# A two-layer graph kernel: copies out of PSUM planned on either of two engines, layer 1's sums put elsewhere, GpSimd's deviations ranked first, and the verdict taken earlier

## The chip, the core and the metric

The kernel runs on one core of one Trainium2 chip. A core has a matrix engine (TensorE, in the profile PE, with its weight loads as PEld), a vector engine (VectorE, DVE), a scalar engine (ScalarE, ACT), a slower general engine (GpSimd, POOL) and SyncE (SP), which here issues nearly all DMA transfers. Each engine works through its own queue in order; semaphores tie the queues together. Matmul results land in PSUM, a small memory[...], from which ScalarE or VectorE copies them to SBUF.

The metric is the device time of one launch in microseconds. It was measured in three runs; separately, one execution was profiled.

## The reference, cut to what matters

There are 3327 nodes with 256 features. Layer 0 makes two steps of top-p attention and of a propagation with the given dense matrix, layer 1 is a graph attention with four heads over the non-zeros of that matrix.

```python
h = jnp.maximum(_layernorm(x, axis=-1), 0.0)
# layer 0, h is X
R = S + jnp.eye(N); R = R / R.sum(-1, keepdims=True)
Xf = X; Xa = X; Z = 0
for n in range(2):
    A = _top_p_attention(Xa, W1, W2, W3)      # softmax, nucleus 0.9, renormalised
    Xf = R @ Xf
    Xa = A @ Xa
    Z = Z + Xf @ U1[n].T + Xa @ U2[n].T
x = x + layernorm(X + Z) * ln_g + ln_b
# layer 1, on h = relu(layernorm(x)):
hp = (h @ W).reshape(n, H, FH)
e = leaky_relu(s[:, :, None] + d[:, None, :], 0.2)   # s, d: hp with the two halves of a
attn = softmax(where(adj > 0, e, -inf), axis=2)
x = x + elu(einsum('hij,jhf->ihf', attn, hp))
```

## The kernel before

The nodes are cut into 26 tiles of 128 rows. Everything is float32. A function `fast` does the work with a quick search for the nucleus threshold, and sets a flag `again` where its assumptions fail; a slow function `general` then runs instead. With the inputs here it does not run.

**How the order comes about.** `fast` does not issue its instructions as it goes. It describes pieces of work to a `Plan`: for each piece an engine, a length in microseconds, a rank, the pieces that it needs, and buffers that it takes and gives back. `Plan.order` (from L496) then walks through a simulated time: each engine, when free, starts that ready piece with the lowest rank whose buffers are free. `Plan.issue` writes the instructions out in the order found, so the order of every engine's queue is fixed when the kernel is built. The chip follows that order; only its waits are found at run time.

**The stages.** First each tile of x is loaded and normalised. `deviations` (from L1133) measures mean and variance on VectorE (L1142, L1143) and takes the reciprocal deviation for a group of one to four tiles on GpSimd (L1147 to L1150); `prepare` applies it on ScalarE (L1168), transposes the tile on TensorE (L1173), copies it (L1176), projects it to keys and queries (L1181), copies that to `kq` (L1187) and spreads it with two GpSimd copies (L1190, L1191) and an SP transfer (L1194). `project_u` (L1220) multiplies each tile by the first layer weights.

Each of the two steps n then does, for each of 26 rows of tiles: logits (L882) and exponentials (L893); a search for the threshold by counting passes over 3327 columns on ScalarE (L930) with small steps on GpSimd or VectorE; a window and sort on VectorE (L985, L990); four drops (L1042); and `attention`: seven groups of up to four transpositions (L1055) into a two-deep PSUM buffer `px`, a copy to SBUF by ScalarE (`Row.turned`, L1060), and matmuls into `acca` (`Row.attend`, L1067). After the first step `finish1`, after the second `finish2`, carry the row on; each turns its result on TensorE and copies it to `xt` by ScalarE (L1242, L1360), and `finish1` copies `kq` (L1251).

Beside this, `Full` multiplies the loaded matrix tiles with the features, 26 matmuls for each row of tiles (L1099), into `accf`. ScalarE copies the sum out (`Full.copy`, L1106), and `Full.add` (L1115) adds the row's own tile on VectorE. In the first step there is one `accf` buffer; in the second there are two, the halves of one PSUM bank. These matmuls depend on no search, so they fill TensorE's time.

Layer 1, `attend_neighbours`, works in four quarters of columns (W = 832). For each of 26 tiles j it makes masks on ScalarE (L1634, L1635), four exponents on VectorE (L1646) into an `e` buffer, and matmuls into PSUM (L1662 for the features, L1676 for the sums). At the end of a quarter `leave` copies the sums out (L1724, L1727) into one of the four `e` buffers, and they are transposed (L1746), divided and stored.

After the plan, written out by hand, the verdict closes: reductions of the failure marks (L1925 to L1929) and two times a copy, a transposition (L1936) and a reduction (L1937), then the flag (L1938). All engines load the flag (L1945) and branch past `general`.

```python
if j == 0 and self.n == 0:
    self.acc = ps_a.tile([P, D + 1], F32, name="accf")
elif j == 0:
    if self.t == 0:
        late["accf"] = ps_a.tile([P, 2, D], F32, name="accf")
    self.acc = late["accf"][:, self.t % 2, :]
```

Of the kernel before, what the change touches and what calls it, by code (L numbers as in the profile page):

```python
# [25 lines left out]
H = 4  # L26
# [443 lines left out]
class Plan:  # L470
# [8 lines left out]
    def put(self, engine, length, rank, fn, *args, needs=(), take=(), give=(), lag=None, hold=0.0):  # L479
# [7 lines left out]
        while stack:  # L487
            q = stack.pop()
            if isinstance(q, dict):
                p["needs"].append(q)  # L490
                q["then"].append(p)
            elif q is not None:
                stack.extend(q)
        self.pieces.append(p)
        return p

    def order(self):
# [11 lines left out]
        for k, p in enumerate(self.pieces):  # L509
            p["k"], p["left"], p["from"] = k, len(p["needs"]), 0.0  # L510
            if not p["left"]:
                ready[p["engine"]].append(p)
        out, clock, holds = [], 0.0, []
        while len(out) < len(self.pieces):
            while events and events[0][0] <= clock:
# [14 lines left out]
                for q in p["then"]:  # L530
                    if (q["engine"] == p["engine"]) == (what == "own"):
                        q["left"] -= 1
                        if not q["left"]:
                            ready[q["engine"]].append(q)
            for e, queue in ready.items():
# [6 lines left out]
                queue.remove(p)  # L542
# [30 lines left out]
def fast(  # L573
# [59 lines left out]
    with ExitStack() as l0:  # L633
# [215 lines left out]
        plan = Plan(dict(rows=1, mvs=3, pl=2, px=2, acca=1, accf=1, accf0=1, accf1=1, et=3, at=4, y=1, e2=3, mask=2, **BUFS))  # L849

        class Row:
# [205 lines left out]
            def turned(self, g):  # L1057
                m = min(4, NT - 4 * g)
                self.et[g] = etpool.tile([P, 4, P], F32, name="et")
                S.copy(self.et[g][:, :m, :], self.pt.pop(g)[:, :m, :])  # L1060
# [16 lines left out]
        class Full:  # L1077


            def __init__(self, n, t):  # L1080
                self.n, self.t, self.at = n, t, {}
                self.src, self.w = (main, D + 1) if n == 0 else (c, D)
                self.bank = f"accf{t % 2}" if n else "accf"
# [6 lines left out]
            def some(self, js):  # L1090
                for j in js:
                    if j == 0 and self.n == 0:
                        self.acc = ps_a.tile([P, D + 1], F32, name="accf")
                    elif j == 0:

                        if self.t == 0:
                            late["accf"] = ps_a.tile([P, 2, D], F32, name="accf")
                        self.acc = late["accf"][:, self.t % 2, :]
# [5 lines left out]
            def copy(self):  # L1104
                self.f = small.tile([P, H * FH + 2 * H], F32, name="f", bufs=BUFS["f"])
                S.copy(self.f[:, : self.w], self.acc[:, : self.w])  # L1106

# [4 lines left out]
            def add(self):  # L1112
                rs = rsum[:, self.t : self.t + 1]
                f, here = self.f[:, :D], c[:, self.t, :]
                V.tensor_add(f, f, self.src[:, self.t, :D])  # L1115
# [17 lines left out]
        def deviations(lo, hi):  # L1133
# [23 lines left out]
            a = plan.put("POOL", 1.1 + 0.2 * m, -100.0 + lo, rest, needs=[a])  # L1157
            return {lo + k: (a, held, k, k == m - 1) for k in range(m)}

        def prepare(t, measured):  # L1160
# [24 lines left out]
            def share():  # L1185
                held["kq"] = small.tile([P, P], F32, name="kq", bufs=BUFS["kq"])
                S.copy(held["kq"], held["ps"])  # L1187
# [9 lines left out]
            a = hs[0][t] = plan.put("ACT", 0.6, r, relu, needs=[ready_], give=["mvs"] * last)  # L1197
            a = plan.put("PE", 0.25, r, turn, needs=[a], take=["pl"])
            a = turned_h[t] = plan.put("DVE", 0.43, r, copy, needs=[a], give=["pl"])
            a = plan.put("PE", 0.5, r, project, needs=[a, weighed], take=["px"])  # L1200
            a = plan.put("ACT", 0.3, r, share, needs=[a], take=["kq"], give=["px"])
# [9 lines left out]
        def project_u(t, rank):  # L1211
# [10 lines left out]
            a = plan.put("PE", 1.75, rank, product, needs=[turned_h[t], uloads], take=[bank])  # L1222
# [5 lines left out]
        def finish1(row, done, rank):  # L1228
# [11 lines left out]
            def copy():  # L1240
                held["xt"] = small.tile([P, 2, P], F32, name="xt")
                S.copy(held["xt"], held["pt"])  # L1242
# [6 lines left out]
            def share():  # L1249
                held["kq"] = small.tile([P, P], F32, name="kq", bufs=BUFS["kq"])  # L1250
                S.copy(held["kq"], held["ps"])  # L1251
# [32 lines left out]
            x_ = plan.put("ACT", 0.3, r, copy, needs=[a], take=["xt"], give=["px", "xa"])  # L1284
            a = plan.put("PE", 0.45, r, project, needs=[x_], take=["px"])
            a = plan.put("ACT", 0.27, r, share, needs=[a], take=["kq"], give=["px"])
# [31 lines left out]
        def finish2(row, done, z, rank):  # L1318
# [39 lines left out]
            def copy():  # L1358
                held["xt"] = small.tile([P, 2, P], F32, name="xt")
                S.copy(held["xt"], held["pt"])  # L1360
# [25 lines left out]
            a = plan.put("POOL", 0.85, r, deviation, False, needs=[a])  # L1386
            a = plan.put("DVE", 1.6, r, second, needs=[a, x_], take=["mv"], give=["mv"], hold=0.95)
            s_ = plan.put("SP", 0.1, r, store, needs=[a])
            a = plan.put("POOL", 1.1, r, deviation, True, needs=[a])
# [3 lines left out]
            a = plan.put("ACT", 0.3, r, copy, needs=[a], take=["xt"], give=["px", "xa"])  # L1393
            a = plan.put("PE", 0.9, r, project, needs=[a], take=["px"])
            a = plan.put("ACT", 0.72, r, stage, needs=[a], take=["f"], give=["px", "xt"])
            return plan.put("DVE", 0.6, r, scale, needs=[a], give=["f"]), s_
# [24 lines left out]
        def search(row, rank, keys, stats_of, fresh):  # L1421
# [4 lines left out]
            for g in range(2):  # L1426

                def logits(g=g):
# [4 lines left out]
                    "PE", 2.0 - 0.8 * g, rank - 2.5, logits, needs=[keys, fresh, a], take=["pl", "pl"] + ["e", "sc"] * (1 - g)  # L1433
# [8 lines left out]
            a = row.pieces["guess"] = plan.put("ACT", 1.0, rank - 2.4, row.guess, needs=[a])  # L1442
# [542 lines left out]
```

## Time and profile before

| | us |
|---|---|
| median of three runs | 2197.55 |
| lowest and highest | 2196.28, 2198.43 |
| the profiled execution, its time | 2193.86 |
| the profiled execution, its span | 2192.1 |
| TensorE busy | 2158.7 |
| VectorE busy | 1605.3 |
| ScalarE busy | 1441.6 |
| GpSimd busy | 926.6 |

The span runs from the first to the last instruction; the time also holds what lies around it. A group row of the profile reads: line, engine, operation, tile written and tiles read, shape, count, then busy time of the group and mean nanoseconds of one, then the idle time of the engine just before these instructions and what ended it. A wait row gives total, number, longest. A timeline row gives start, length, engine, line, and in brackets the idle time before it. A float32 matmul appears as two records. The ends of matmuls are modelled, so a busy TensorE can hide short refills.

### The profile page before, as it was taken

To read this page: it belongs to the slowest core of one execution; us is meant where nothing else is said; L and a number is where in the kernel's file an instruction comes from. 1 tells how busy PE (TensorE), PEld (TensorE's weight loads), DVE (VectorE), ACT (ScalarE), POOL (GpSimd) and SP (SyncE) were. 2 spreads that over 40 slices of the span, in tenths; PEclk is the share of its full clock that TensorE was granted. 3 is DMA by queue.
4 is the path that set the end of the run, shared out by engine and by line. 5 is a ranking of instruction groups with operands and counts; after the bars stand their busy time and mean duration, and the time that the engine had idled before them with its cause. 6 is when DMAs were issued, how large, how long until landed. Compare 5 with 4: busy or idle time off the path is not lost. (4 is left out here: it accounts for less than half of the span.)

```text
span 2192.1 us, 35711 instructions
## 1 busy us (share of the span) xinstructions
PE 2158.7 (98%) x11872; PEld 1519.1 (69%) x11872; DVE 1605.3 (73%) x4205; ACT 1441.6 (66%) x2714; POOL 926.6 (42%) x2259
## 2 busy tenths in 40 slices
PE   8999999999999999999999999999999999999997
PEld 6578778778787788777778777878788433333332
DVE  5567666657556571367998888788878898989896
ACT  5786776667666742578888787788673556465553
POOL 5466565546533550265666665656563100000001
PEclk9999999999999999999999999999999999999999
DMA  4012122222222233532222222222124534444341
GB/s 121 21 36 85 48 63 62 64 72 64 57 58 62 72 116 92 154 95 58 63 59 64 59 74 61 75 75 69 56 72 136 157 114 145 119 137 127 110 127 53
DMA packets 192323, 183.74 MB, mean 84 GB/s; under 512 B 15386, under 2 KB 146176, under 8 KB 192128
## 3 DMA queue, kind: packets, MB, share of 16 engines
q1 hardware_dynamic: 191232, 181.15, 28.4%
q8 instruction: 95, 1.56, 0.3%
q14 instruction: 100, 0.82, 0.1%
q10 hardware_dynamic: 896, 0.21, 0.0%
HBM read 164.41 MB, written 15.94 MB: 82 GB/s over the span
## 5 line engine op out<-in xcount | busy, mean ns | idle before, releaser
L1067 PE MATMUL acca<-rhs,et 128*128 128x256 f32 x2704 | 618.2, 379 | 0.1
L930 ACT ACTIVATE junk<-e,sc 128x3327 fp8e5<-128x3327 f32 x182 | 558.8, 3070 | 81.4 <-POOL sc L975 81.0
L1067 PEld LDWEIGHTS acca<-rhs,et 128*128 128x128 f32 x2704 | 498.3, 190 | 61.8 <-issue 1.8
L1099 PE MATMUL accf<-c,at 128*128 128x256 f32 x1352 | 316.1, 383 | 6.3 <-ACT f L1106 5.7
L985 DVE SCALAR_TENSOR_TENSOR y<-e,sc 128x1664 f32<-128x1664 f32 x104 | 204.8, 1969 | 152.6 <-POOL sc L972 150.3
L1099 PE MATMUL accf<-main,at 128*128 128x257 f32 x1352 | 309.8, 381 | 1.5 <-ACT f L1106 1.5
L1099 PEld LDWEIGHTS accf<-c,at 128*128 128x128 f32 x1352 | 249.2, 190 | 54.1 <-issue 10.6
L1099 PEld LDWEIGHTS accf<-main,at 128*128 128x128 f32 x1352 | 251.4, 190 | 46.1 <-issue 8.1
L1060 ACT COPY et<-px 128x512 f32<-128x512 f32 (+1 forms) x364 | 192.6, 553 | 119.5 <-PE acca L1067 62.9
L990 DVE MAX8 cands<-y 128x8 f32<-128x208 f32 x832 | 242.2, 361 | 3.6
L1042 DVE SCALAR_TENSOR_TENSOR e<-e,thr 128x832 f32<-128x832 f32 x208 | 212.9, 1081 | 2.0
L893 ACT ACTIVATE e<-pl 128x1024 f32<-128x1024 f32 x208 | 179.9, 869 | 43.3 <-PE pl L882 43.3
L1635 ACT ACTIVATE et<-at 128x448 bf16<-128x448 f32 (+1 forms) x204 | 112.3, 550 | 131.9 <-DVE e L1646 74.2
L1798 POOL TENSOR_TENSOR qq<-qq 128x256 f32<-128x256 f32 x4 | 3.0, 757 | 461.2 <-ACT qq L1794 461.1
L1055 PE MATMUL px<-ident,e 128*128 128x128 f32 x1352 | 191.9, 274 | 6.0 <-ACT et L1060 3.5
L1055 PEld LDWEIGHTS px<-ident,e 128*128 128x128 f32 x1352 | 160.1, 141 | 50.0 <-issue 13.5
L1662 PE MATMUL pl<-e,main 128*64 128x416 f32 x1024 | 192.5, 517 | 0.3
L882 PE MATMUL pl<-kt,qq 64*128 64x512 f32 (+1 forms) x832 | 173.7, 536 | 0.8 <-ACT e L893 0.8
L1662 PEld LDWEIGHTS pl<-e,main 128*64 128x64 f32 x1024 | 70.9, 137 | 113.3 <-issue 86.4
L1646 DVE SCALAR_TENSOR_TENSOR e<-c,low,et 128x832 f32<-128x832 f32 x128 | 128.6, 1070 | 12.0 <-PE accf L1676 10.4
L882 PEld LDWEIGHTS pl<-kt,qq 64*128 64x128 f32 x832 | 71.5, 186 | 84.4 <-issue 77.3
L1646 DVE SCALAR_TENSOR_TENSOR e<-qq,low,et 128x832 f32<-128x832 f32 x120 | 120.4, 1072 | 6.0 <-PE accf L1676 4.4
(534 smaller groups left out, 3032.3 us busy)
## 6 DMA issues: line engine op xcount, KB each, us to landing
at<-in_adjt_dram SPq DMA_DIRECT2D x414, 256.0 KB
at<-in_adjt_dram SPq DMA_DIRECT2D x102, 192.0 KB
at<-in_adjt_dram SPq DMA_DIRECT2D x52, 128.0 KB
ys<-ystage SPq DMA_DIRECT2D x26, 256.0 KB
rhs<-in_x_dram SPq DMA_DIRECT2D x26, 128.0 KB
ystage<-in_x_dram SPq DMA_DIRECT2D x26, 128.0 KB
base<-ys SPq DMA_DIRECT2D x26, 128.0 KB
x1s<-ystage SPq DMA_DIRECT2D x26, 128.0 KB
```

What stands on the lines that cost most here:

```text
L882: T.matmul(pl[:, lo : lo + m], qq[half, self.i, :], kt[half, 512 * k : 512 * k + m], start=True, stop=True,)
L893: S.activation(self.e[:, 1024 * k : 1024 * k + pl.shape[1]], pl, AF.Exp, accum_out=(self.p0, self.p1, self.p2, self.p3)[k],)
L930: S.activation(junk[:, :N], self.e[:, :N], fn, bias=t, scale=-1.0, accum_out=dst, saturate=False)
L985: V.scalar_tensor_tensor(self.y[:, : hi - lo], self.e[:, lo:hi], self.up, self.e[:, lo:hi], ALU.is_lt, ALU.mult, accum_out=(self.h0, self. ...
L990: V.max(self.cands[:, o // PIECE, :], self.y[:, o - lo : min(o + PIECE, hi) - lo])
L1042: V.scalar_tensor_tensor(piece, piece, self.thr[:, o : o + 1], piece, ALU.is_gt, ALU.mult)
L1055: T.transpose(pt[:, k, :], self.e[:, j * P : (j + 1) * P], ident)
L1060: S.copy(self.et[g][:, :m, :], self.pt.pop(g)[:, :m, :])
L1067: T.matmul(self.acc, et[:, j - 4 * g, :], rhs[self.n][:, j, :], start=(j == 0), stop=(j == NT - 1))
L1099: T.matmul(self.acc[:, : self.w], self.at[j // JC][:, j % JC, :], self.src[:, j, : self.w], start=(j == 0), stop=(j == NT - 1),)
L1646: V.scalar_tensor_tensor(held["e"][:, k, :], extra["both"][b % 2][:, k, :], low[:, j, k : k + 1], held["mask"], ALU.max, ALU.mult,)
L1662: T.matmul(q["acc"][a][k * FH : (k + 1) * FH, c, :C], main[:, j, h * FH : (h + 1) * FH], held["e"][:, h, c * C : (c + 1) * C], start=(j == 0),
```

## The change

Most copies out of PSUM become pieces that two engines can do: `Plan.either` gives a length and a function for each of ScalarE and VectorE, and the walk through simulated time gives the piece to whichever engine gets to it first. This holds for the transposed tiles, for `xt` in `finish1` and `finish2`, for `kq` in `finish1` and for the sums of `Full`; for the last, VectorE's variant `take` adds the row's own tile in the same instruction. The copies of `kq` in `prepare` stay on ScalarE.

The second step's `accf` becomes one buffer. The rank of GpSimd's deviations goes from -100 to -180. Layer 1's sums leave PSUM into `y` (free since the last search) and the memory of `kt`, and take no `e` buffer. The verdict becomes three pieces of the plan with ranks that fall into the last quarter, with one transposition where there were two. Some thirty lengths of pieces are changed, among them those of the steps, the guess, the windows and the exponents.

```diff
+        p["on"] = {engine: (length, fn, p["lag"], hold)}
         self.pieces.append(p)
+        return p
+
+    def either(self, first, second, rank, *args, **kw):
+
+        p = self.put(*first[:2], rank, first[2], *args, **kw)
+        p["on"] = {e: (length, fn, self.LAG[e], 0.0) for e, length, fn in (first, second)}
+        p["engine"] = ""
         return p
...
                 p = min(can, key=lambda q: q["rank"])
-                queue.remove(p)
+                for k in p["on"]:
+                    ready[k].remove(p)
+                p["engine"] = e
+                p["length"], p["fn"], p["lag"], p["hold"] = p["on"][e]
...
-            def turned(self, g):
+            def turned_by_s(self, g):
+                self.turned(g, S.copy)
+
+            def turned_by_v(self, g):
+                self.turned(g, V.tensor_copy)
+
+            def turned(self, g, copy):
                 m = min(4, NT - 4 * g)
                 self.et[g] = etpool.tile([P, 4, P], F32, name="et")
-                S.copy(self.et[g][:, :m, :], self.pt.pop(g)[:, :m, :])
+                copy(self.et[g][:, :m, :], self.pt.pop(g)[:, :m, :])
...
-                    if j == 0 and self.n == 0:
-                        self.acc = ps_a.tile([P, D + 1], F32, name="accf")
-                    elif j == 0:
-
-                        if self.t == 0:
-                            late["accf"] = ps_a.tile([P, 2, D], F32, name="accf")
-                        self.acc = late["accf"][:, self.t % 2, :]
+                    if j == 0:
+                        self.acc = ps_a.tile([P, self.w], F32, name="accf")
...
+            def take(self):
+                self.f = small.tile([P, H * FH + 2 * H], F32, name="f", bufs=BUFS["f"])
+                V.tensor_add(self.f[:, :D], self.acc[:, :D], self.src[:, self.t, :D])
+                if self.n == 0:
+                    V.tensor_copy(self.f[:, D : D + 1], self.acc[:, D:])
+                self.added = True
...
-                V.tensor_add(f, f, self.src[:, self.t, :D])
+                if not self.added:
+                    V.tensor_add(f, f, self.src[:, self.t, :D])
...
-            a = plan.put("POOL", 1.1 + 0.2 * m, -100.0 + lo, rest, needs=[a])
+            a = plan.put("POOL", 1.25 + 0.19 * m, -180.0 + lo, rest, needs=[a])
...
-            x_ = plan.put("ACT", 0.3, r, copy, needs=[a], take=["xt"], give=["px", "xa"])
+            x_ = plan.either(
+                ("ACT", 0.3, copy), ("DVE", 0.43, lambda: copy(V.tensor_copy)), r, needs=[a], take=["xt"],
+                give=["px", "xa"],
+            )
...
-                a = plan.put("DVE", 2.7, rank - 1.3, row.step, 2, V, needs=[a])
+                a = plan.put("DVE", 3.35, rank - 1.3, row.step, 2, V, needs=[a])
...
-                b = plan.put("ACT", 0.03 + 0.115 * m, rank - 2.6, row.turned, g, needs=[b], take=["et"], give=["px"])
+                b = plan.either(
+                    ("ACT", 0.06 + 0.105 * m, row.turned_by_s), ("DVE", 0.12 + 0.135 * m, row.turned_by_v),
+                    rank - 2.6, g, needs=[b], take=["et"], give=["px"],
+                )
...
-                    take=[f.bank] * (j == 0) + ["accf"] * (n == 1 and t + j == 0), give=["at"] * last,
+                    take=["accf"] * (j == 0), give=["at"] * last,
                 )
-            a = plan.put(
-                "ACT", 0.3, -90.0, f.copy, needs=[a], take=["f"],
-                give=[f.bank] + ["accf"] * (n == 1 and t == NT - 1),
+            a = plan.either(
+                ("ACT", 0.35, f.copy), ("DVE", 0.45 + 0.12 * (n == 0), f.take), -90.0, needs=[a], take=["f"],
+                give=["accf"],
             )
...
-                        q["ot"] = epool.tile([P, NP], F32, name="e")[:, : 3 * W].rearrange("p (k c w) -> p k c w", k=3, c=2)
+                        q["ot"] = scr.tile([P, 2 * W], F32, name="y").rearrange("p (k w) -> p k w", k=2)
+                        q["ot"] = [q["ot"][:, 0], q["ot"][:, 1]]
                     if k < 2:
-                        S.copy(q["ot"][:, k], q["acc"][k][:, :, :C])
+                        S.copy(q["ot"][k].rearrange("p (c w) -> p c w", c=2), q["acc"][k][:, :, :C])
                     else:
+                        if "den" not in extra:
+                            extra["den"] = wpool.tile([P, 2 * W], F32, name="kt")[:, :W]
+                        q["ot"].append(extra["den"])
...
+        def gather_rows():
+            late["pr"] = ps_x.tile([1, P], F32, name="px")
+            T.transpose(late["pr"], far[:, 0:1], ident)
+
+        def tell():
+            V.tensor_reduce(verdict[:, 0:1], late["pr"], AX.X, ALU.max)
+            V.tensor_tensor(again, verdict[:, 0:1], verdict[:, 0:1], ALU.max)
+
+
+        a = plan.put("DVE", 1.5, 92.0, judge, needs=[[a for a, _ in ends], failed])
+        a = plan.put("PE", 0.15, 92.1, gather_rows, needs=[a], take=["px"])
+        plan.put("DVE", 0.45, 92.2, tell, needs=[a], give=["px"])
         plan.issue(tc)
```

## The prediction

> **What bounds the kernel now.** I read the totals first, then busy time by stage, then TensorE's own waits, then the timeline at the two kinds of wait that recur. The totals:
>
> ```profile
> span 2192.1 us, 35711 instructions
> PE 2158.7 (98%) x11872; PEld 1519.1 (69%) x11872; DVE 1605.3 (73%) x4205; ACT 1441.6 (66%) x2714; POOL 926.6 (42%) x2259
> ```
>
> TensorE is busy in all but 33.4 us of the span, at a granted clock of 0.997. The change takes one 128x128 transposition from TensorE and adds none, so the matmul stream itself, some 2159 us, stays. Whatever is won must come out of the 33.4 us, or from small refills that a busy figure hides. Where the idle time lies, by stage (columns: stretch; length; busy time of TensorE, weight loads, VectorE, ScalarE, GpSimd; clock; DMA):
>
> ```profile
> core 0: us, PE busy (x) PEld busy (x) DVE busy (x) ACT busy (x) POOL busy (x), PEclk, DMA share, GB/s
> 0.00:34.00 34.00, 27.12 (x162) 22.04 (x163) 22.02 (x77) 19.25 (x51) 23.98 (x85) 0.95 0.52 152
> ...
> 95.00:150.00 55.00, 53.26 (x279) 41.27 (x278) 40.77 (x148) 45.03 (x89) 36.23 (x79) 1.00 0.18 50
> 150.00:800.00 650.00, 648.46 (x3257) 517.38 (x3256) 405.26 (x1173) 450.54 (x788) 350.71 (x851) 1.00 0.23 66
> ...
> 915.00:1710.00 795.00, 783.77 (x3967) 637.45 (x3965) 643.34 (x2074) 602.95 (x1030) 459.52 (x1108) 1.00 0.25 72
> 1710.00:2176.00 466.00, 465.66 (x3384) 169.79 (x3384) 429.82 (x488) 249.50 (x595) 4.53 (x5) 1.00 0.43 124
> 2176.00:2192.10 16.10, 4.90 (x35) 2.47 (x27) 7.35 (x24) 6.18 (x16) 6.14 (x7) 0.71 0.18 59
> ```
>
> So: opening 6.9 us idle, 95 to 150 us 1.7, first step 1.5, second step (915 to 1710) 11.2, layer 1's quarters 0.3, end 11.2. TensorE's waits name the releasers:
>
> ```profile
> PE accf L1099 <- ACT f L1106: 7.2, 13, 1.1
> PE pl L1173 <- ACT rhs L1168: 3.6, 3, 2.5
> PE px L1055 <- ACT et L1060: 3.5, 2, 3.2
> ...
> PE px L1055 <- DVE e L1042: 1.1, 3, 0.6
> PE px L1055 <- DVE gk L789: 1.1, 1, 1.1
> ```
>
> The first and third rows are copies out of PSUM that ScalarE makes late. Two stretches show the form, TensorE first:
>
> ```profile
> 961.95 1.89 PE L1067 MATMUL acca<-rhs,et 128*128 128x256 f32 x8
> 963.68 1.03 PE L1099 MATMUL accf<-c,at 128*128 128x256 f32 x4
> 965.17 1.13 PE L1099 MATMUL accf<-c,at 128*128 128x256 f32 x4 [0.46 <-ACT f L1106]
> ```
> ```profile
> 1562.85 3.07 ACT L930 ACTIVATE junk<-e,sc 128x3327 fp8e5<-128x3327 f32 x1 [5.39 <-POOL sc L975]
> ...
> 1565.91 0.56 ACT L1060 COPY et<-px 128x512 f32<-128x512 f32 x1
> ```
>
> Eight matmuls take 961.95 to 963.68, 0.216 us each. The next four take 1.49 us where 0.86 would do: 0.63 lost (0.46 of it shown as idle). The new row of tiles writes the other half of the same bank, and still TensorE waits for the copy of the old half. In the second stretch a copy stands behind a 3.07 us count; TensorE waited 3.2 us.
>
> **The change part by part.**
>
> 1. *The sums' copy (L1106) and one buffer in the second step.* The order of the two builds shows 9 of 25 boundaries between rows of tiles in the second step with no other matmul between before, 3 after; the rest now have at least four. Before, the waits there are 7 of 0.46, 2 of 0.69 and 1.10 at 917 us, 5.7 in all. After: 3 x 0.46 = 1.4, where the three are copy 0.37 plus hand-over. Saved 4.3; and 0.17 of refill (0.63 less 0.46) at some six boundaries, 1.0. Of 52 copies 15 go to VectorE as an add straight from PSUM, which takes the place of the 0.42 us add that VectorE made anyway (two cost 0.15 more for the row sum's column in the first step): VectorE's load does not grow by them.
>  Here the Trainium skill speaks against the change: "Trace Analysis", section Optimizing Tensor Performance, Matmuls, has independent matmul groups rotate through PSUM banks, so that the copy of one lies beside the next group's matmuls. The change takes the second buffer away. By the rule every boundary would now show its copy, 0.46, and 25 of them 11.5 us, against none with rotation. By the row the two halves never rotated in effect, and the single buffer of the first step, with matmuls of other rows between, shows only 1.5 us for 26. I take the row.
>
> 2. *Transposed tiles (L1060) by either engine.* 139 of 364 copies go to VectorE (120 of 128x512, 19 of 128x256; 80 of the 139 in the second step), with 12 and 6 copies of xt and 8 of kq. The trace has no 128x512 copy on VectorE. From its PSUM copies of 64 columns (222 ns) and 256 (417 ns, L1176), 1.02 ns a column: 0.68 us, an estimate; bounds 0.42 (no cost beyond 256) and 0.83 (two of 256). ScalarE takes 584 ns. VectorE gains 120 x 0.68 + 37 x 0.42 + 8 x 0.28, about 99 us; ScalarE sheds about 92. Both lie beside TensorE. In the second step VectorE goes from 643 to about 643 + 57 = 700 of 795 us (88%), ScalarE from 603 to about 550. What is queued behind such a copy on VectorE is a row's window, sort and drops, for which that row's transpositions wait. In the new order, copies standing right behind a count on ScalarE fall from 78 of 364 to 36 of 225, and of L1106 from 28 of 52 to 11 of 37. Gain: the 3.2 us hole, and at 95 to 150 us two holes of 0.83 and 0.91 in which a copy or exponential stood behind a count: 1.4 of 1.7. In the first step 0.4 (one wait for L1106); the 1.1 for L789 stays, VectorE's own queue. Added: late drops, 0.5; and if the 165 moved copies are exposed as ScalarE's 364 were (3.5 us, 0.010 each), 1.6.
>  The unknown is how often a copy on VectorE comes late: never at best, and at worst often enough for rival three.
>
> 3. *Deviations first on GpSimd.* At the opening a group of three deviations (L1147 to L1150) ran at 17.40 behind three pairs of key copies that waited for ScalarE's kq; its inputs were there by 14.4. After, one pair stands ahead of it, done at 15.15. Its relu (19.26), and the transposition behind the 2.51 us hole, come 2.2 earlier. Keys and their kq buffers are freed up to 1.8 later per group; SP's copies of kq do not pass GpSimd. Gain 2.2, from 0 (the hole moves to the keys, which the first logits need, 51.8 us) to 4. In the new order 6 instead of 9 products L1220 stand ahead of those logits: less filler should a key be late.
>
> 4. *Layer 1's sums in y and kt.* The transposed sums no longer hold one of four e buffers. TensorE is idle 0.34 us in 1710 to 2176, so at most 0.3; I take 0. VectorE's waits there cost nothing while TensorE is full.
>
> 5. *Verdict in the last quarter.* Its five reductions (369, 149, 154, 196, 161 ns), one transposition and two small operations run under TensorE, with 36 us free on VectorE in that stage. Removed: two copies (150 each), a transposition, a reduction, and the wait: all five engines' loads of the flag start at 2185.9, right after the verdict's last write. TensorE's branch then takes 4.35 us to 2190.9, while SP branches at 2187.1 and reports from 2190.1. After, TensorE is free from 2181.6 and leaves the chain; SP, whose flag load now stands ahead of its last stores, branches after its last store at about 2185.9: 1.2, with 0.1 of VectorE's reduction ahead of the last quotient: 1.3. The output stores themselves stay.
>
> 6. *Lengths of the planner:* no instruction, only order; changes of row mode on TensorE number 1,141 in both.
>
> **Sum.** Opening 2.2, 95 to 150 us 1.4, first step 0.4, second step 4.3 + 1.0 + 3.2 - 0.5 = 8.0, end 1.3: 13.3; less 1.6 for new waits: 11.7, say 12. The profiled execution took 2193.86 (span 2192.1), below the runs shown (2196.28 to 2198.43). It would take 2181.9, with a span near 2180; the median 2197.55 becomes **2185.5**.
>
> **Rivals.**
>
> One: nearly all idle time before the last matmul goes but the 1.8 ahead of the first one. 33.4 less 9.5 behind the last matmul leaves 23.9; 19 of it and 1.3 at the end make 20: 2177.5. For it: the planner's lengths come closer to the rows (a window's first half, 1.95 + 1.2, was planned at 3.2, now 3.12; step three at 2.7 now 3.35). Against: VectorE's late drops stay.
>
> Two: the choice of engine is made when the plan is built, not when an engine is free; holes move and don't shrink. For it: the plan's fixed places, as all the waits above came out of a plan too. Gain 0 to 4, about 2195.5.
>
> Three, the other sign: VectorE in the second step. A copy there sits behind a 1.95 us window operation or a 3 us step in a queue that is 88% full; two px buffers hang on it, and TensorE, in order, stands still. Price: 139 copies; from 0.09 us exposed each the gain is gone (12.5), from 0.12 it is slower than can be taken for noise. At 0.15 (21 us): 2206. Against: ScalarE, 76% full, exposed 0.010.
>
> **How the numbers follow.** Forecast 0.70 (own range 2179 to 2192), rival one 0.11, two 0.09, three 0.10. The range reaches from 2177 to 2196: it leaves out rival three, half of two and part of one. A difference of 0.2% is 4.4 us, about what can be told from none. Faster: forecast, one, and a fifth of two, 0.83; same 0.07; slower 0.10.
>
> **What would show it.** TensorE's idle time in the second step from 11.2 to about 4; its wait for L1106 from 7.2 to about 2 in total; no wait over 3 us for a transposed copy; the hole at 17 us under 0.5; flag loads of the engines at different times, TensorE's branch over by 2187 on the old time axis. It is wrong if waits of TensorE for VectorE's copies sum to over 5 us, or if VectorE stays under 670 us in the second step. Also wrong if the 128x512 copy on VectorE takes over 0.83.

## The result, and the profile after

The changed kernel takes **2187.09 us** (median of five runs, 2184.67 to 2188.23), the kernel before in the same session 2198.01. The ratio is 0.9951, with a 95% interval of 0.9941 to 0.9962: 10.9 us gained, 11.7 to 12 forecast. The profiled execution took 2188.23 us with a span of 2186.3, only 5.8 below the span of before. That is less than the medians differ by, since the profiled execution of before lies below its median and this one above.

The totals of the page, and busy time by stage (columns as before):

```profile
span 2186.3 us, 35745 instructions
...
PE 2157.4 (99%) x11871; PEld 1518.6 (69%) x11871; DVE 1698.1 (78%) x4372; ACT 1371.5 (63%) x2534; POOL 946.0 (43%) x2259
```
```profile
0.00:34.00 34.00, 26.08 (x146) 21.35 (x147) 21.32 (x77) 18.05 (x45) 22.06 (x78) 0.90 0.51 149
34.00:95.00 61.00, 59.56 (x233) 32.24 (x232) 27.09 (x107) 34.33 (x85) 22.35 (x69) 1.00 0.09 26
95.00:150.00 55.00, 53.08 (x278) 41.03 (x277) 37.19 (x132) 39.22 (x74) 31.45 (x76) 1.00 0.15 43
150.00:800.00 650.00, 648.88 (x3251) 514.93 (x3250) 449.62 (x1268) 424.82 (x729) 352.49 (x850) 1.00 0.23 66
...
915.00:1710.00 795.00, 790.77 (x4009) 642.02 (x4009) 697.57 (x2167) 569.19 (x939) 486.92 (x1120) 1.00 0.26 75
```

TensorE's idle time in the second step fell from 11.2 to 4.2 us. In the opening (0 to 95 us) it rose: 7.9 + 1.4 = 9.4, where before had 6.9 + 0.3 = 7.1. TensorE's waits (total, times, longest) say where:

```profile
PE px L1203 <- ACT kq L1209: 5.0, 2, 3.6
PE accf L1112 <- ACT f L1119: 2.0, 3, 1.0
PE pl L1195 <- ACT rhs L1190: 1.9, 3, 1.1
...
PE accf L1112 <- DVE f L1124: 1.8, 2, 1.3
```

The sums' copy (L1119 on ScalarE, L1124 on VectorE; L1106 before) is waited for 3.8 us in place of 7.2. The wait of 3.2 us for a transposed tile is gone; its row is down from 3.5 to 0.2. The first row grew most: ScalarE's copies of keys are waited for 5.0 us, where before had 0.3.

Idle time alone misleads here, as one stage shows more than its idle time can give. So every trace was cut at four places: the start of the first matmul of the sums in the first step, the start of the first of those in the second step, the end of the last of those, and the end of layer 1's last feature matmul. "Quarters" lies between the last two.

| us | opening | first step | second step | quarters | rest | second step + quarters |
|---|---|---|---|---|---|---|
| before | 95.4 | 822.2 | 791.2 | 465.3 | 18.0 | 1256.4 |
| changed | 99.9 | 821.6 | 785.0 | 461.5 | 18.4 | 1246.5 |

So 9.9 us come from the last two stages: 6.2 from the second step, **3.7 from the quarters**, where TensorE had only 0.34 us of idle time. The opening gives some back.

### The profile page after: what moved, and what is told of

The parts are those of the page before. It is cut to its first block, busy times and chain, and to the rows that moved or that the text cites. A ratio compares the mean times of both kernels' runs of the same rounds, so it can differ in the third digit from the quotient of the medians.

```text
span 2186.3 us, 35745 instructions
## 1 busy us (share of the span) xinstructions
PE 2157.4 (99%) x11871; PEld 1518.6 (69%) x11871; DVE 1698.1 (78%) x4372; ACT 1371.5 (63%) x2534; POOL 946.0 (43%) x2259
## 3 DMA queue, kind: packets, MB, share of 16 engines
q1 hardware_dynamic: 191232, 181.15, 28.6%
q8 instruction: 95, 1.56, 0.3%
## 5 line engine op out<-in xcount | busy, mean ns | idle before, releaser
L1112 PEld LDWEIGHTS accf<-c,at 128*128 128x128 f32 x1352 | 249.4, 190 | 48.4 <-issue 10.5
L1079 ACT COPY et<-px 128x512 f32<-128x512 f32 (+1 forms) x225 | 122.2, 552 | 161.2 <-PE acca L1086 99.4
L1079 DVE COPY et<-px 128x512 f32<-128x512 f32 (+1 forms) x139 | 88.8, 647 | 77.7 <-PE px L1068 58.4
```

What stands on the lines that cost most here:

```text
L1112: T.matmul(self.acc[:, : self.w], self.at[j // JC][:, j % JC, :], self.src[:, j, : self.w], start=(j == 0), stop=(j == NT - 1),)
```

## The experiments

Twelve kernels ran; the kernel before in those sessions has medians of 2196.59 to 2197.49. Each was executed five times or more, and the ratios are to the kernel before.

**Which part pays? Four edits of the changed kernel.** First, the deviations get their old rank:

```diff
-            a = plan.put("POOL", 1.25 + 0.19 * m, -180.0 + lo, rest, needs=[a])
+            a = plan.put("POOL", 1.25 + 0.19 * m, -100.0 + lo, rest, needs=[a])
```

> The changed kernel with the rank of GpSimd's deviations put back from -180 to -100 (its lengths kept). Theory A (the deviations, taken first, pile up key copies whose three kq buffers wait for SP): TensorE's idle time from 0 to 95 us falls from 9.4 us to about 7, ScalarE's wait for SP's copies of kq from 7.8 to under 3, and the time falls by about 2 us against the changed kernel. Theory B (the opening is worse because other pieces moved, fewer products ahead of the first logits): idle time from 0 to 95 us stays at 9 or more, time unchanged within 1 us.

Then x is loaded in pairs from the seventh tile on, deviations first as in the change:

```diff
-            nc.sync.dma_start(rhs[0][:, t, :], x[t * P : (t + 1) * P, :])
+            if t < PAIRED:
+                nc.sync.dma_start(rhs[0][:, t, :], x[t * P : (t + 1) * P, :])
+            else:
+                nc.sync.dma_start(
+                    rhs[0][:, t : t + 2, :], x[t * P : (t + 2) * P, :].rearrange("(a p) d -> p a d", p=P)
+                )
```

> The changed kernel with x loaded in pairs of tiles from tile 6 on: 16 transfers on SP's queue where there were 26, so that SP comes to the copies of kq some 4 us sooner than 16.3 us. Theory A: the wait of ScalarE for kq's copies falls from 7.8 to under 4 us, TensorE's idle time from 0 to 95 us from 9.4 to about 6, time lower by about 3 us. Theory B: idle time to 95 us stays within 1 us of 9.4. A third way, a pair lands later than a single tile: VectorE's wait for x grows by more than 2 us and takes the gain.

Then every two-engine piece gets ScalarE's variant alone:

```diff
-        p["on"] = {e: (length, fn, self.LAG[e], 0.0) for e, length, fn in (first, second)}
+        p["on"] = {e: (length, fn, self.LAG[e], 0.0) for e, length, fn in (first,)}
```

> The changed kernel with every copy of the two-engine pieces on ScalarE alone; one accf buffer, lengths and the rest as changed. Theory A (VectorE's share of the copies is what took the waits of TensorE for copies out of the second step): TensorE's idle time from 915 to 1710 us rises from 4.2 to about 8 and the time by about 4 us. Theory B (one buffer with other matmuls between, and truer lengths, did it): idle time there stays under 6, time within 1.5 us of the changed kernel.

And last, the second step gets its two halves of `accf` again:

```diff
-                        self.acc = ps_a.tile([P, self.w], F32, name="accf")
+                            late["accf"] = ps_a.tile([P, 2, D], F32, name="accf")
+                        self.acc = late["accf"][:, self.t % 2, :]
```

> The changed kernel with the second step's sums again in the two halves of one bank, planned as two buffers. Theory A (the planner believes in the second half, puts nothing between two rows of tiles, and TensorE waits for the copy all the same): waits of TensorE for the sums' copy rise from 3.8 to about 7 us, time up by 3 to 4 us. Theory B (halves make no difference once either engine can copy): waits within 1 us of 3.8, time within 1 us.

Measured: deviations late 2184.29 us (0.995, 0.9936 to 0.9963), pairs 2184.44 (0.9946, 0.9932 to 0.996), ScalarE alone 2197.28 (1.0004, 0.9995 to 1.0012), two halves 2185.24 (0.9953, 0.994 to 0.9967). The first two shorten the opening in their traces (the first sums start at 96.5 and 97.7 us, changed 99.9; ScalarE waits 5.6 and 3.8 us for the copies of keys, changed 7.8; TensorE is idle 7.6 and 7.8 us up to 95 us, changed 9.4), but by time they can't be told from the changed kernel. Two halves do as well as one buffer (TensorE waits 4.8 us for the sums, changed 3.8), so the single buffer is not what pays. Without VectorE's share the whole gain is gone, more than the 4 us expected: TensorE is idle 13.6 us in the second step. By this run the free choice of engine looks like the whole gain.

**Single parts on the kernel before.** That reading was put to the test by adding one part at a time. The free choice of engine alone (old lengths, two halves):

```diff
-            a = plan.put(
-                "ACT", 0.3, -90.0, f.copy, needs=[a], take=["f"],
+            a = plan.either(
+                ("ACT", 0.35, f.copy), ("DVE", 0.45 + 0.12 * (n == 0), f.take), -90.0, needs=[a], take=["f"],
```

and in the same way for the tiles, `xt` and `kq`.

> The kernel before with one part of the change alone: tiles of weights, xt, kq and the rows' sums are copied out of PSUM by ScalarE or VectorE as the plan finds either free. Two halves of accf, GpSimd's old order, the old lengths of all other pieces and the old verdict stay. Theory B (the free choice is the whole gain): TensorE's idle time from 915 to 1710 us falls from 11.2 to 4 or 5 us, waits for the sums' copy from 7.2 to below 5 in total, time 8 to 10 us below before, about 2187.5. Theory C (the choice needs the new lengths beside it, since a plan with wrong lengths puts the copies in the wrong places): idle time there 7 to 10 us, gain 1 to 4 us.

Measured: 2211.93 us, ratio 1.007 (1.0056 to 1.0084). Fifteen us **slower**. That the choice needs the lengths beside it was right in kind, but the gain of 1 to 4 us that went with it was not. The largest of five holes that TensorE has in this second step, as a timeline of all engines:

```profile
1536.14 3.07 ACT L943 ACTIVATE junk<-e,sc 128x3327 fp8e5<-128x3327 f32 x1 [5.00 <-POOL sc L988]
...
1536.24 0.69 DVE L1079 COPY et<-px 128x512 f32<-128x512 f32 x1 [0.22 <-PE px L1068]
...
1540.21 0.57 ACT L1079 COPY et<-px 128x512 f32<-128x512 f32 x1
...
1540.83 1.54 PE L1068 MATMUL px<-ident,e 128*128 128x128 f32 x6 [3.77 <-ACT et L1079]
```

ScalarE had nothing to do for 5.00 us while it waited for a threshold step on GpSimd; only then could its count begin, and the copy that the plan had put behind the count and an exponential came four us late. The plan gives a copy to the engine that is free first, but first in its own simulated time, and that time does not hold here.

One buffer alone, and the verdict alone:

```diff
-                        self.acc = late["accf"][:, self.t % 2, :]
+                        self.acc = ps_a.tile([P, self.w], F32, name="accf")
```

> The kernel before with one buffer for the rows' sums in place of two halves of one bank, and nothing else; all copies stay with ScalarE. The prediction's step (one buffer makes the plan put other matmuls between the rows): TensorE waits for the sums' copy 1.4 to 2 us in place of 7.2, gain 4 to 5 us. The rule of rotated buffers: 25 boundaries of 0.46 us show, the wait becomes about 11.5, loss 4 to 6 us. What the run of two halves in the changed kernel suggests: neither, within 1.5 us of before.

```diff
+        a = plan.put("DVE", 1.5, 92.0, judge, needs=[[a for a, _ in ends], failed])
+        a = plan.put("PE", 0.15, 92.1, gather_rows, needs=[a], take=["px"])
+        plan.put("DVE", 0.45, 92.2, tell, needs=[a], give=["px"])
         plan.issue(tc)
```

> The kernel before with the verdict's pieces in the plan, in the last quarter, and nothing else. The prediction's step: 1.3 us less between the end of the last matmul of layer 1 and the end of the span (18.0 us before), time about 2195.5. What the changed kernel's trace suggests (SyncE's own chain sets the end: its last store, its branch, and some 3.5 us behind it): the end stays within 0.5 us, no difference in time.

One buffer: 2204.34 us, 1.004 (1.0027 to 1.0054), slower. TensorE's waits in that run:

```profile
PE accf L1094 <- ACT f L1101: 8.9, 13, 1.3
PE px L1055 <- ACT et L1060: 4.1, 2, 3.4
...
PE acca L1067 <- ACT et L1060: 3.0, 1, 3.0
```

The wait for the sums is 1.7 longer than before, and a hole of 3.0 us for a transposed tile is new. The rule has the sign right, and the row of the first step, on which the prediction relied, has not.

The order of TensorE's matmuls in this trace says why. The plan did put other work between the rows of tiles: of the 25 boundaries in the second step, 9 had no other matmul between in the kernel before, and 4 have none here. These four wait 0.46 to 1.34 us, 2.9 together. But five boundaries with four or eight matmuls between wait as well, 0.46 to 0.99 us, 3.3 together, as the copy itself comes late. It begins 2.0 to 3.3 us after the row's last matmul, in four of the five right behind a count, as in this one (four transpositions lie between):

```profile
983.27 3.07 ACT L930 ACTIVATE junk<-e,sc 128x3327 fp8e5<-128x3327 f32 x1 [1.83 <-POOL sc L975]
...
986.33 0.35 ACT L1101 COPY f<-accf 128x256 f32<-128x256 f32 x1
...
986.74 1.13 PE L1094 MATMUL accf<-c,at 128*128 128x256 f32 x4 [0.99 <-ACT f L1101]
```

The verdict alone: 2196.46 us, 0.9998 (0.999 to 1.0006), nothing, and the rest behind the last matmul is 18.0 us as before.

**The lengths.** Sixteen lengths of the opening and the steps, alone and then with the free choice; layer 1 stays as before in both. Four of them against the trace of the kernel before, each from the first start to the last end of its instructions: the guess takes 1.56 us (planned 1.0, now 1.46), the piece behind it 0.61 (0.85, now 0.55), the third step on VectorE 3.42 (2.7, now 3.35), the failure marks 3.04 (2.2, now 2.95).

```diff
-            a = row.pieces["guess"] = plan.put("ACT", 1.0, rank - 2.4, row.guess, needs=[a])
-            more = plan.put("ACT", 0.85, rank - 2.2, row.density, needs=[a])
+            a = row.pieces["guess"] = plan.put("ACT", 1.46, rank - 2.4, row.guess, needs=[a])
+            more = plan.put("ACT", 0.55, rank - 2.2, row.density, needs=[a])
...
-                a = plan.put("DVE", 2.7, rank - 1.3, row.step, 2, V, needs=[a])
+                a = plan.put("DVE", 3.35, rank - 1.3, row.step, 2, V, needs=[a])
```

> The kernel before with the new lengths of the planner's pieces in the opening and the two steps (16 of them), and nothing else; all copies stay with ScalarE, two halves of accf, the old quarters. Theory L (lengths nearer to the measured ones are what lets the plan put copies in the right places, with one engine as with two): TensorE's idle time from 915 to 1710 us falls from 11.2 to 7 or less, time 3 to 6 us below before. Theory B+L (lengths pay only where there is a choice of engine): idle time there 10 to 14 us, time within 2 us of before. Theory R (every edit of the plan reshuffles it, and a few holes of 1 to 4 us fall by luck): any value from 5 below to 8 above.

> The kernel before with the free choice of the copying engine and those 16 lengths; two halves of accf, GpSimd's old order, the old quarters and the old verdict stay. Theory B+L: the choice alone cost 15 us and the lengths turn it: idle time from 915 to 1710 us about 4 us, no hole over 1.5 us there, second step with quarters 1249 us or less (1256.4 before, 1246.5 in the changed kernel), time 7 to 9 us below before, about 2189. Theory R: second step with quarters between 1250 and 1270, at least one hole over 2 us, no gain or a loss.

Measured: lengths alone 2191.87 us, 0.9976 (0.9965 to 0.9987); with the choice 2188.97, 0.9962 (0.9948 to 0.9975). The windows of the second step, lengths alone first:

```profile
915.00:1710.00 795.00, 787.59 (x3998) 641.43 (x3999) 649.45 (x2081) 608.16 (x1036) 480.93 (x1116) 1.00 0.26 75
```
```profile
915.00:1710.00 795.00, 790.99 (x4028) 641.37 (x4030) 694.96 (x2157) 574.87 (x956) 482.13 (x1115) 1.00 0.27 76
```

TensorE is idle 7.4 us with ScalarE copying everything, and 4.0 with the choice, where before had 11.2. With two halves of `accf`, a plan whose lengths come nearer needs no second engine for most of the gain. Holes over 0.7 us in the second step: two before, five with the choice alone, four with lengths alone (the longest 1.21), none with choice and lengths. For lengths alone theory L holds in the stage (-6.8 us) and in the time (-5.6), with the idle time a little over its mark of 7; "lengths pay only with a choice" falls. That chance alone decides (theory R) is not excluded by two runs. The last run below fits the lengths too; but no run moved the lengths away from the measured ones, so that some other plan might do as well stays open.

**Layer 1's buffers alone:**

```diff
-                        q["ot"] = epool.tile([P, NP], F32, name="e")[:, : 3 * W].rearrange("p (k c w) -> p k c w", k=3, c=2)
+                        q["ot"] = scr.tile([P, 2 * W], F32, name="y").rearrange("p (k w) -> p k w", k=2)
+                        q["ot"] = [q["ot"][:, 0], q["ot"][:, 1]]
```

> The kernel before with the transposed sums of layer 1 in the y and kt buffers, and nothing else. The prediction's step: at most 0.3 us. What the two traces suggest (VectorE waits 14.7 us in four places for TensorE to release an e buffer, the longest 4.4; in the changed kernel 0.6): these waits fall below 2 us, the stretch from the ninth matmul of the first quarter to the last matmul of layer 1 falls from 463.9 to about 461.7 us, time 2.2 us below before. If the old lengths of the exponents' pieces cause these waits instead, they stay and the time does too.

Measured: 2193.57 us, 0.9982 (0.9975 to 0.9989): 3.9 us, almost twice what was expected here. VectorE's waits in the quarters, before and then in this run:

```profile
DVE e L1646 <- PE accf L1676: 14.7, 4, 4.4
```
```profile
DVE e L1646 <- PE accf L1676: 0.9, 1, 0.9
```

The stretch from the ninth matmul of the first quarter to the last of layer 1 fell from 463.9 to 459.7 us. The time is won in the last three quarters, some 32 us after each begins: between the 528th, 944th and 1360th matmul of the features and the ones 104 later it takes 28.6, 28.6 and 29.0 us before, and 27.4 each time here. In the changed kernel they take 27.4 as well. The first four microseconds of the first of these stretches, before and then in this run:

```profile
1855.75:1859.75 4.00, 3.92 (x19) 1.48 (x16) 4.00 (x5) 1.84 (x4) 0.00 (x0) 1.00 0.78 219
```
```profile
1857.93:1861.93 4.00, 4.00 (x32) 1.47 (x32) 4.00 (x5) 2.04 (x4) 0.00 (x0) 1.00 0.41 114
```

TensorE starts 19 matmul records in place of 32 and yet shows 3.92 of 4 us as busy. VectorE, whose exponents these matmuls take, is busy throughout: it had lost time to the waits for a buffer, and its tiles come late.

**A better opening, and the last test of the lengths.** The changed kernel with x in fours from the seventh tile on and the old rank of the deviations:

```diff
-            nc.sync.dma_start(rhs[0][:, t, :], x[t * P : (t + 1) * P, :])
+            m = 1 if t < ALONE else 4
+            nc.sync.dma_start(
+                rhs[0][:, t : t + m, :], x[t * P : (t + m) * P, :].rearrange("(a p) d -> p a d", p=P)
+            )
```

> The changed kernel with two edits at the opening: from the seventh tile on x is loaded in fours, 11 loads in place of 26 on SyncE's queue, and the deviations on GpSimd have their old rank. If SyncE's queue is what keeps the kq buffers full: its first copy of kq is issued before 13 us (16.3 in the changed kernel), ScalarE's wait for these copies falls from 7.8 us to below 3, the first full product starts at 96 us or earlier (99.9), time 4 us below the changed kernel, about 2183. If four tiles in one load land too late: TensorE waits for the deviations' tiles instead, idle time before 34 us above 8, time as the changed kernel or above.

Measured: **2181.83 us**, 0.9934 (0.9921 to 0.9948). It beats both kernels: each of its five executions (2181.61 to 2182.68) lies below each of the changed kernel's. The first sums start at 94.5 us (99.9 in the changed kernel). SyncE's first copy of keys leaves at 14.9 us, not before 13: the loads on SyncE's queue are over by 12.1, but ScalarE has copied the first keys only at 14.6. ScalarE waits 4.9 us for the copies on SyncE, not under 3. So the size of the gain fits and the step is only half as clean as expected. From this kernel, ScalarE alone and two halves again (the two edits shown above):

> The kernel of the run with x in fours (deviations late), with two further edits: ScalarE alone makes all copies, and the sums have two halves of accf again. New lengths, layer 1's buffers and the verdict in the plan stay. Theory L (the new lengths carry the gain of the second step; the free choice of engine only makes up for what the single buffer costs): second step with quarters 1245 to 1248 us, as with the choice (1246.9), time within 3 us of 2181.8, so that half of the change can be left out. Theory B (VectorE's share of the copies is the gain): 1255 to 1258 us, as in the run with ScalarE alone and one buffer (1257.0), time 2190 to 2193.

Measured: 2182.29 us, 0.9933 (0.992 to 0.9947), as fast as with the choice. Its second step, all copies on ScalarE:

```profile
915.00:1710.00 795.00, 789.40 (x4015) 639.20 (x4017) 651.94 (x2083) 606.28 (x1037) 465.26 (x1110) 1.00 0.26 76
```

Theory L holds: the free choice and the single buffer can be left out together. The last two stages were expected at 1245 to 1248 us and took 1248.6, so the choice may be worth one to three.

The cuts side by side (us; second step, quarters, their sum):

| lengths of the steps | free choice | buffers | second step | quarters | sum |
|---|---|---|---|---|---|
| old (before) | no | two | 791.2 | 465.3 | 1256.4 |
| old (one buffer alone) | no | one | 796.4 | 465.2 | 1261.6 |
| old (choice alone) | yes | two | 806.0 | 465.0 | 1271.0 |
| old, layer 1's buffers new (layer 1's buffers alone) | no | two | 791.2 | 461.0 | 1252.3 |
| new (lengths alone) | no | two | 784.4 | 466.2 | 1250.6 |
| new (choice and lengths) | yes | two | 783.1 | 466.2 | 1249.2 |
| new, layer 1's part too (ScalarE alone, fours) | no | two | 785.5 | 463.1 | 1248.6 |
| new, layer 1's part too (ScalarE alone) | no | one | 795.2 | 461.8 | 1257.0 |
| new, layer 1's part too (two halves) | yes | two | 782.9 | 462.9 | 1245.8 |
| new, layer 1's part too (changed) | yes | one | 785.0 | 461.5 | 1246.5 |

Each row is one profiled execution. The second step took 791.2 to 791.9 us in three traces that have the same order of the sums' matmuls there (before, verdict alone, layer 1's buffers alone), and 784.8 to 785.1 in four (changed, deviations late, pairs, fours), so a difference under 1 us says nothing.

The choice of engine is worth 10.5 us where there is one buffer (1257.0 to 1246.5), and 1.4 to 2.8 where there are two. The lengths, too, have no worth of their own: in the second step they win 6.8 us with two buffers (791.2 to 784.4), 22.9 with the choice as well (806.0 to 783.1), and next to nothing with one buffer and ScalarE alone (796.4 to 795.2, with the other new parts beside them). The run with ScalarE alone had therefore been misread: taking VectorE away exposed the single buffer, and the loss of the one was put down as the gain of the other.

## Why the prediction was right, point by point

The time was right within 1.6 us. So were TensorE's idle time in the second step (4.2 us, about 4 forecast) and VectorE's load there. The wait for the sums was 3.8 us where about 2 stood, and the hole at 17 us was to fall under 0.5 but was 1.07, with a new one of 3.64 behind it. **The sum was right by its total, not by its terms, and that their errors cancelled is luck.**

1. *One buffer, -5.3.* Wrong. The wait for the sums fell to 3.8 us, not about 2, and not through this part: alone it costs 7.5 us in time, with the new lengths and ScalarE alone it costs too (table), with the choice it is worth nothing. The step that failed is "I take the row": the row of the first step showed that a single buffer *can* be hidden, not that this plan would hide it. "After: 3 x 0.46" took only the boundaries without matmuls between as waiting, and the copy as prompt. With one buffer alone boundaries with matmuls between waited 3.3 us, for copies that stood behind other work on ScalarE. In the changed kernel, where VectorE can take the copy, only the three empty boundaries wait, 2.5 us in place of 1.4. The nine and three boundaries were read from an order in which all parts had worked together.
2. *Tiles by either engine, -3.2 in the second step, +0.5 and +1.6 against.* The parts that could be measured fit. A 128x512 copy takes 684 ns on VectorE (0.68 estimated), and VectorE came to 697.6 us in the second step (700). The group rows of that copy in the changed kernel, VectorE and ScalarE:

```profile
L1079 DVE COPY et<-px 128x512 f32<-128x512 f32 x120 | 81.1, 684 | 73.5 <-PE px L1068 58.4 <-PE acca L1086 14.7 <-issue 0.2
```
```profile
L1079 ACT COPY et<-px 128x512 f32<-128x512 f32 x192 | 110.1, 584 | 134.9 <-PE acca L1086 76.7 <-PE px L1068 55.4 <-DVE sc L964 1.7
```

   The waits of TensorE for VectorE's copies, 1.8 for sums and 0.6 for tiles, stay under 5 us, so rival three did not happen. The 1.4 us put down for 95 to 150 us did not come: TensorE was idle 1.7 us there before, and 1.9 after. Alone the part makes the kernel 15 us slower, by what rival two said, though it allowed no loss: the choice is fixed when the plan is built, and holes move. The late copies were ScalarE's, not VectorE's.
3. *Deviations first, -2.2.* No gain, and most likely a loss. The group's relu came earlier (15.97 against 19.26 us) and the 2.51 us hole shrank to 1.07, but a hole of 3.64 us opened for the keys, the "0" end of the range and beyond. The timeline of the changed kernel:

```profile
13.08 0.41 ACT L1209 COPY kq<-px 128x128 f32<-128x128 f32 x2
...
15.88 0.28 POOL L1212 COPY kt<-kq 64x128 f32<-64x128 f32 x1
...
16.29 8.11 SPq L1216 DMA_DIRECT2D qq<-kq  x7
...
20.87 0.27 ACT L1209 COPY kq<-px 128x128 f32<-128x128 f32 x1 [3.32 <-DMA qq<-kq]
```

   Keys lie ready at 13.1, but SyncE is busy with the loads of x and u until 16.2, before as after; three `kq` buffers fill, and TensorE stands. "SP's copies of kq do not pass GpSimd" was true and beside the point: they hang on SyncE's own queue, and the earlier tiles ran into it. How much it costs is less sure. The same opening took 95.4, 98.8, 98.3 and 97.8 us in four executions (before, verdict alone, one buffer, layer 1's buffers); with deviations first it took 99.9, 99.4 and 99.0, and 96.5 with the old rank in the changed kernel. Part of this scatter goes with the granted clock (last section). With the same mean clock of 0.95 in the first 34 us, the old rank took 95.4, 96.5 and 96.8 us (before, deviations late, choice alone), the new one 99.4 and 99.0 (ScalarE alone, two halves): about 3 us, by few samples, and not shown by the time of a whole run.
4. *Layer 1's buffers, 0.* Wrong: 3.9 us. "TensorE is idle 0.34 us, so at most 0.3" is the failed term. These matmuls have records of 0.51 us that start 0.17 us apart, so a start can slip by some 0.3 us before idle time shows: 19 records in place of 32 still gave 3.92 of 4 us busy (windows above). The prediction had said this of refills and not used it here; VectorE's 14.7 us of waits for a buffer stood in the profile.
5. *Verdict, -1.3.* Nothing. TensorE's branch did leave the chain (over by 2179.9), but SyncE's own took its place. With the verdict alone SyncE branched 0.86 us earlier after the last matmul (12.19 against 13.05), and its next event came 3.87 us later, where it had been 3.05.
6. *Lengths, "only order".* The largest error. Alone they win 5.8 us in the last two stages, where the whole change wins 9.9. The order was read for what it showed, and the cause was looked for in the parts with instructions. Equal counts of changes on TensorE, the sign that the prediction took, do not say where a wait falls.

By the runs, on one way through the table: lengths -5.8 us, layer 1's buffers -4.1, the choice beside the lengths -1.4 (1250.6 to 1249.2), one buffer +0.7 (1245.8 to 1246.5): -10.6 in the last two stages, if parts simply added; measured -9.9. Another way would share it out differently, and the last of these parts is within the scatter. By stage, the second step gave 6.2 of its 8.0, the opening, the stretch to 150 us and the end nothing of their 2.2, 1.4 and 1.3, and the quarters 3.7 that no term had. Which of the sixteen lengths matter was not tried. Nor were layer 1's new lengths tried apart.

## What to carry over

Where a planner fixes the order, a part of a change is worth what the plan makes of it: a freer choice in a plan with wrong lengths cost 15 us, and 16 better numbers alone won 5.6. A buffer can be spared where its copy comes soon, and other work in between does not help where the copy waits behind a 3 us count. Removing a part from the finished kernel does not show what the part is worth if another part leans on it; add it alone as well, and fill the table. And an engine's idle figure is no ceiling for a gain where late inputs only spread the starts of its work; measure the stage from start to start, and look at the waits of the engine that feeds it.

## What was not expected of the hardware

**A hole can cost more than its length.** After the 3.77 us hole shown above (free choice alone), TensorE was granted half its clock for more than 5 us; windows of that run:

```profile
1536.00:1541.00 5.00, 1.23 (x7) 0.78 (x6) 3.40 (x12) 4.86 (x7) 2.95 (x6) 0.86 0.17 52
1541.00:1545.00 4.00, 4.00 (x16) 3.52 (x17) 3.72 (x11) 3.02 (x14) 1.09 (x3) 0.50 0.02 4
1545.00:1549.00 4.00, 4.00 (x17) 3.43 (x16) 0.76 (x3) 3.97 (x3) 0.00 (x0) 0.82 0.29 78
1549.00:1553.00 4.00, 4.00 (x20) 3.51 (x20) 2.53 (x7) 2.20 (x2) 0.41 (x2) 1.00 0.61 184
```

The clock is 0.50 in the first four microseconds behind the hole, 0.82 in the next: some 2.7 us lost (4 x 0.50 + 4 x 0.18) beside the 3.77. The changed kernel's 3.64 us hole in the opening has the same (0.52 from 21 to 25 us), and so has a 2.95 us hole of the run with the choice alone (0.50 from 1684 to 1688). The 3.23 us hole of before had none (1.00 from 1564 on), nor had one of 3.45 us with one buffer. One and the same hole goes either way: it is 3.21 us long both with the verdict alone and with layer 1's buffers alone, and the windows behind it are, in this order:

```profile
1570.00:1574.00 4.00, 4.00 (x21) 3.66 (x20) 3.59 (x11) 2.76 (x9) 0.00 (x0) 0.65 0.02 6
```
```profile
1569.00:1573.00 4.00, 4.00 (x27) 3.69 (x27) 3.58 (x13) 3.33 (x11) 0.00 (x0) 1.00 0.08 17
```

The Trainium skill, "TensorE: Matmul & The Clock Gate", part 1, has the clock halved after an idle window of about 3.4 us, and the window runs free of the kernel's start. That would let a hole of 3.45 us go either way, but not one of 2.95 or 3.21 us, unless the modelled ends of matmuls make these look shorter than they are; here the measured clock decides. The wait rows show none of this cost.

**The opening scatters.** The four executions of the same opening (before, verdict alone, one buffer, layer 1's buffers) had mean granted clocks of 0.95, 0.85, 0.90 and 0.90 in the first 34 us, the fastest with the highest. One profile of an opening does not settle 2 us.
